# Holding GpSimd's work of a step behind the comparison of hi, and dealing the features into 20 turns over ten steps

## The chip, the cores and the metric

One core of one Trainium2 chip. The metric is the device time of one execution in microseconds (us), the median of the runs shown. The work is laid on five engines: TensorE (PE), VectorE (DVE), ScalarE (ACT), GpSimd (POOL) and SyncE (SP), the last of which here only issues DMAs.

## What is computed

Thirty-two images of 128 channels by 1024 tokens go through two layers. Cut to what matters:

```python
out = chunk_attention(q=ctx, k=ctx, v=ctx) * mask + x      # 8 heads, chunks of 64 tokens
x1 = (out - mean(out)) * rsqrt(var(out) + 1e-5)            # over the tokens
# second layer: 30 nearest neighbours of each token by ctx[:, 0:3]
idx = top_k(-squared_distance(ctx3, ctx3), 30)
rel = ctx3[idx] - ctx3                                     # 3 coordinates
rho   = sqrt(max(x*x + y*y + z*z, 1e-20))
theta = arctan2(z, sqrt(max(x*x + y*y, 1e-20)))
phi   = arctan2(y, x)
h = three small linear layers, each with batch norm over all images and a leaky relu
out = x1 + sum over neighbours of softmax(h) * x1[idx]
```

## The kernel before

The kernel has three parts. **Part 1** does the attention, the normalization, the search for the neighbours, and the angles of each neighbour ("features"). Part 2 is the three small layers, which need statistics over all images. Part 3 weights and sums the neighbours. The change is in part 1 alone.

Part 1 is a software pipeline over steps. An image has eight tiles of 128 tokens (NJ = 8), so there are S = 256 steps, and `step(s)` (L887) works on several tiles at once: the search of tile s (`distances_copy`, `eight`), the spreading of the indices of tile s-1 (`spread_indices`, with its DMAs), the comparison and gather of tile s-2 (`onehot`, `evicted`), the selection of tile s-3 (`masked`, `summed`), and the coordinates of tile s-4 (`found`, `relative`). Eleven short steps drain it. I call s modulo 8 the *phase* of a step. All of part 1 stands under `written_order`: each engine runs its instructions in the order in which the program wrote them, so a wait of one instruction holds up all that follows on its engine. Tiles come from pools with one to three buffers, and a write waits for the last reader of the buffer.

On **DVE** a step is: the maximum of the scores (L498), `eight(s, 0)`, the comparison of hi (L688), `eight(s, 1)`, a reciprocal (L510), the extras planned for s-0.5, `eight(s, 2)`, the extras planned for s, and `eight(s, 3)`. One `eight` is MAX8, FIND_INDEX8 and, but for the last, MATCH_REPLACE8 (L639 to L642) on 128x1024 float32. The comparison is one `tensor_scalar` on 128x4096 bf16, in place in the tile `hb`: the high parts of all indices of a tile against the partition's number.

On **GpSimd** a step is: `masked(s-3)` (L724, two multiplications of 128x512), `relative(s-4)` (L749, which waits for ACT's copy `got`, L742), the multiplication by the reciprocal in `normalize(s)` (L511), then the extras. `masked` needs nothing of its own step, so it starts when the extras of the step before are done.

On **ACT** a step is: eight exponentials (L502), the splitting of the indices, the copies of distances (L630), `lows` (L707, L708), copies of PSUM results, `got`, the extras of s-0.5, the copies `mk` (L714), and the extras of s.

The extras are planned by step number (L857 to L885), t0 = 8b being the first step of image b, and an x.5 means the first of the two places of a step. Among them on GpSimd: `residual` (L558, L559) in phases 5 and 1, `mask_bias` (L426) in phase 4, `norm_step` (L586 to L590) in phase 5, `split_squares` and `split_channels` (small casts and subtractions) in phase 3. On ACT: `project` (L460 and eight times L465) in phases 5 and 1, `values` (L451) and `transposed` (L609) in phase 6. On DVE: `moments1` (L565) in phases 6 and 2.

`features(b)` (L755) is a generator whose pieces, "turns", are planned one by one. Its element-wise work runs on GpSimd (on DVE for the last image), its logarithms, exponentials, sign and arctangent on ACT, and two operations with two tensor inputs (`V.scalar_tensor_tensor`, L795 and L796) and six statistics (L835, L838) on DVE. ACT loads a table wherever neighbouring instructions of its order need different ones (ACT_TABLE_LOAD). In the kernel before, 13 turns lie at t0+11.5 to t0+17.5.

Of the kernel before, what the change touches and what calls it, by code (L numbers as in the profile page):

```python
# [12 lines left out]
BF16 = mybir.dt.bfloat16  # L13
F16 = mybir.dt.float16
AF = mybir.ActivationFunctionType
ALU = mybir.AluOpType
# [7 lines left out]
TINY = 1e-20  # L24
# [31 lines left out]
def kernel(ctx: ExitStack, tc: tile.TileContext, aps: dict, out: bass.AP):  # L56
# [12 lines left out]
    nc = tc.nc  # L69
    x_d, ctx_d, mask_d = aps["x"], aps["ctx_4096"], aps["mask_Bx1x4096_ff1"]  # L70
    B, C, T = x_d.shape
# [37 lines left out]
    left = NEG  # L109
    for _ in range(3):  # L110
        m, e = math.frexp(left)
# [43 lines left out]
    least_side = column("least_side", 1e-18)  # L155
    nought_up = column("nought_up", 1e-30)
# [169 lines left out]
    with ExitStack() as part:  # L326
        p1 = part.enter_context(tc.tile_pool(name="p1", bufs=1))
        p2 = part.enter_context(tc.tile_pool(name="p2", bufs=2))
# [355 lines left out]
        def onehot(s):  # L684

            oh, lb = near[s]
            tp = per[s // NJ]["tp"]
            nc.vector.tensor_scalar(oh, oh, pcol, None, ALU.is_equal)  # L688
            pgs = []
            for r in range(2):  # L690
                pg = ps_g.tile([P, 512], F32, tag="g", name=f"ps_g_{s}_{r}")
                for i in range(3):
                    for e in range(4):
                        nc.tensor.matmul(  # L694
                            pg[e * 32 : (e + 1) * 32, :],
                            tp[:, i, :],
                            oh[:, e * 1024 + r * 512 : e * 1024 + (r + 1) * 512],
                            start=(i == 0),
                            stop=(i == 2),
                        )  # L700
                pgs.append(pg)
            near[s] = (lb, pgs)

        def lows(s):

# [13 lines left out]
        def masked(s):  # L719

            lb, mk = near[s]
            for r in range(2):
                half = mk[:, r * 4 : r * 4 + 4, :].rearrange("p k n -> p (k n)")
                nc.gpsimd.tensor_mul(half, half, lb[:, r * 512 : (r + 1) * 512])  # L724
# [30 lines left out]
        def features(b):  # L755

            rel = per[b]["rel"]
            ft = lambda tag: p1.tile([P, 2, E], F32, tag=f"f_{tag}", name=f"f_{tag}_{b}")
            half = lambda tag: p1.tile([P, E], F32, tag=f"h_{tag}", name=f"h_{tag}_{b}")

            V, G = nc.vector, nc.gpsimd if b < B - 1 else nc.vector
            sph = p2.tile([P, 3, E], F32, tag="sph", name=f"sph_{b}")
            sqr = p1.tile([P, 3, E], F32, tag="f_sqr", name=f"f_sqr_{b}")
            nc.scalar.activation(sqr, rel, AF.Square)
            ax, fy, ay = ft("ax"), ft("fy"), ft("ay")
            nc.scalar.activation(ax[:, 1, :], rel[:, 0, :], AF.Abs)
            nc.scalar.copy(fy[:, 0, :], rel[:, 2, :])
            nc.scalar.copy(fy[:, 1, :], rel[:, 1, :])
            nc.scalar.activation(ay, fy, AF.Abs)
            s2 = ft("s2")  # L770
            G.tensor_add(s2[:, 1, :], sqr[:, 0, :], sqr[:, 1, :])
            G.tensor_add(s2[:, 0, :], s2[:, 1, :], sqr[:, 2, :])
            vv, inv = ft("vv"), ft("inv")
            G.tensor_scalar(vv, s2, TINY, None, ALU.max)
            yield
            left = half("left")
            nc.scalar.activation(inv, vv, AF.Ln, scale=1024.0)
            G.tensor_scalar(left, rel[:, 0, :], 0.0, None, ALU.is_lt)
            G.tensor_scalar(s2, s2, TINY, None, ALU.is_ge)
            yield  # L780
            nc.scalar.activation(inv, inv, AF.Exp, scale=-0.5, bias=log_less)

            rr, d = ft("rr"), ft("d")
            G.tensor_mul(rr, vv, inv)
            G.tensor_mul(d, rr, rr)
            G.tensor_sub(d, vv, d)
            yield
            G.tensor_mul(d, d, inv)
            G.tensor_scalar(d, d, 0.5, None, ALU.mult)
            G.tensor_add(sph[:, 0, :], d[:, 0, :], rr[:, 0, :])  # L790

            G.tensor_add(ax[:, 0, :], d[:, 1, :], rr[:, 1, :])
            yield
            big, least, inv = ft("vv"), ft("rr"), ft("inv")
            V.scalar_tensor_tensor(big, ay, 0.0, ax, ALU.max, ALU.max)  # L795
            V.scalar_tensor_tensor(least, ay, -GONE, ax, ALU.min, ALU.min)  # L796
            nc.scalar.activation(fy, fy, AF.Sign, scale=1e20, bias=nought_up)
            nc.scalar.activation(inv, big, AF.Ln, bias=least_side)
            swap = ft("d")
            G.tensor_sub(swap, ay, ax)  # L800
            G.tensor_scalar(swap, swap, 0.0, None, ALU.is_gt)
            yield
            nc.scalar.activation(inv, inv, AF.Exp, scale=-1.0)
            t, e = ft("ay"), ft("ax")
            G.tensor_mul(t, least, inv)
            yield

            G.tensor_mul(e, t, big)
            G.tensor_sub(e, least, e)
            G.tensor_mul(e, e, inv)  # L810
            yield
            G.tensor_add(t, t, e)
            nc.scalar.activation(t, t, AF.Arctan)
            yield
            turn = ft("vv")
            G.tensor_scalar(turn, t, -2.0, PI / 2, ALU.mult, ALU.add)
            G.tensor_mul(turn, turn, swap)
            G.tensor_add(t, t, turn)
            yield
            back = half("back")  # L820
            G.tensor_scalar(back, t[:, 1, :], -2.0, PI, ALU.mult, ALU.add)
            G.tensor_mul(back, back, left)
            G.tensor_add(t[:, 1, :], t[:, 1, :], back)
            G.tensor_mul(t, t, fy)
            yield
            G.tensor_mul(sph[:, 1:3, :], t, s2)
            nc.sync.dma_start(sph_d[b].rearrange("c (p e) -> p c e", e=E), sph)
            sums = []
            for i, (u, v) in enumerate(PAIRS):
                s = p1.tile([P, E], F32, tag=f"h_s{i}", name=f"h_s{i}_{b}")  # L830
                G.tensor_add(s, sph[:, u, :], sph[:, v, :])
                sums.append(s)
            yield
            for c in range(3):
                V.bn_stats(st1[:, c, b, :], sph[:, c, :])  # L835
            yield
            for i, s in enumerate(sums):
                V.bn_stats(st1[:, 3 + i, b, :], s)  # L838

        per, proj, pairs, outs, norms, near, feats = {}, {}, {}, {}, {}, {}, {}  # L840


        extras = {}
# [1 line left out]
        def plan(step, f, *args):  # L845
            extras.setdefault(step, []).append((f, args))
# [8 lines left out]
            next(feats[b], None)  # L855

        S = B * NJ  # L857
        for b in range(B):
            t0 = b * NJ
            if b > 0:  # L860
                plan(t0 - 7, load_ctx, b)
                plan(t0 - 6, load_mask, b)
                plan(t0 + 1, load_rest, b)
                plan(t0 - 6, squares, b)
                plan(t0 - 5.5, sum_squares, b)
                plan(t0 - 5, split_squares, b)
                plan(t0 - 5, split_channels, b)
                plan(t0 - 4.5, turn_squares, b)
                plan(t0 - 4, mask_bias, b)
                plan(t0 - 3, project, b, 0)  # L870
                plan(t0 - 2, values, b)
            plan(t0 + 1, project, b, 1)
            for h in range(NH):
                done = t0 + 4 * h + 4
                plan(done, attended, b, h)
                plan(done + 1, residual, b, h)
                plan(done + 2, moments1, b, h)
            plan(t0 + 10.5, norm1, b)
            plan(t0 + 12, norm_log, b)
            plan(t0 + 12.5, norm_root, b)  # L880
            plan(t0 + 12.5, norm_step, b)
            plan(t0 + 13.5, norm4, b)
            plan(t0 + 14, transposed, b)
            for i in range(13):
                plan(t0 + 11.5 + i / 2, turn, b)  # L885

        def step(s):  # L887
            now = 0 <= s < S
            past = lambda lag: 0 <= s - lag < S
# [8 lines left out]
                spread_indices(s - 1)  # L898
            if now:
                eight(s, 0)  # L900
            if past(3):
                masked(s - 3)
            if past(1):
                turned(s - 1)
            if 0 <= s and s + 1 < S:
# [3 lines left out]
            if past(2):  # L909
                lows(s - 2)  # L910
                onehot(s - 2)
            if past(1):
                attend(s - 1)
            if past(4):
# [49 lines left out]
    with ExitStack() as part:  # L964
# [59 lines left out]
        half = NR // 2  # L1024
# [67 lines left out]
        with written_order(tc):  # L1092
# [12 lines left out]
            a2, s2 = norm(1, 1, *moments(1, 1, st2, CQ, avg_c[:, 0:CQ]), *bn2_h)  # L1105
# [28 lines left out]
    for i in range(2):  # L1134
        t = r1.tile([P, NJ, SL], F32, tag=f"pad{i}", name=f"pad{i}")
        nc.gpsimd.memset(t, 0.0)
        pads.append(t)
    for i in range(3):
        t = r1.tile([P, 4, 3, 32, NJ], BF16, tag=f"apart{i}", name=f"apart{i}")
# [114 lines left out]
    for t in range(NT):  # L1254
        b, j = t // NJ, t % NJ
# [10 lines left out]
        oh, bm = built.pop(t)  # L1266
# [58 lines left out]
```

## Time and profile before

| | us |
|---|---|
| median of 3 runs (5752.46 to 5762.36) | 5760.63 |
| the profiled execution | 5763.89 |
| its span, first to last instruction | 5762.2 |
| part 1, to the start of the last comparison of hi | 4287 |
| the drain of part 1 and the first statistics of part 2 | 58 |
| the rest of part 2, and part 3 | 1417 |
| DVE busy in part 1 | 4197 of 4287 |
| GpSimd busy in part 1 | 2331 |
| ACT busy in part 1 | 3185 |
| PE busy in part 1 | 2957 |

The profile gives the busy time of each engine, groups of equal instructions with their mean duration, and a timeline. A line of the timeline has the start in us from the span's start, the duration in us, the engine, the source line, the operation, what it writes and reads, and, in brackets, the idle time of the engine ahead of it with what ended it. The number after "x" counts instructions merged into the line. In part 1 the picture repeats image by image: from step 100 to step 108, for example, the comparisons of hi start at 1687.16, 1703.03, 1719.40, 1737.59, 1754.28, 1770.15, 1787.19, 1804.40 and 1820.28.

### The profile page before, as it was taken

The page shows a single profiled execution, that of the slowest core. Times are in us where ns is not written, and L with a number is a line of the kernel's source. Part 1 is how long each engine was busy: PE and PEld are TensorE (multiplying, and loading weights), DVE is VectorE, ACT ScalarE, POOL GpSimd, SP SyncE. Part 2 cuts the span into 40 slices and gives each one's busy share as a digit, 9 for nine tenths or more (in the row PEclk, how much of TensorE's full clock was granted, in tenths as well). Part 3 has the DMA queues.
Part 4 walks back from the last instruction along what each step waited for, and adds up shares of the span by engine and source line. Part 5 has one row for each costly group of instructions (what it writes and reads, how often), then busy time and mean ns, then how long its engine had stood idle before and what let it go on. Part 6 is the DMA issues. An engine that isn't in the chain of part 4 may idle for free. (4 is left out here: it accounts for less than half of the span.)

```text
span 5762.2 us, 126784 instructions
## 1 busy us (share of the span) xinstructions
PE 4292.3 (74%) x48908; PEld 2586.3 (45%) x48908; DVE 5289.5 (92%) x6988; ACT 4077.1 (71%) x10116; POOL 2352.9 (41%) x2725
## 2 busy tenths in 40 slices
PE   6776666776766766766776766666758679999999
PEld 3433333433333333333433334333334257777776
DVE  8999999999999999999999999999975598888876
ACT  5777777777777777777777777777764476666664
POOL 3455555555555555555555555555550000000000
PEclk8778878787878878878788878888869689999999
DMA  2222332222223322332332223323322133333332
GB/s 77 103 102 103 113 106 100 106 106 98 104 103 106 106 100 102 115 103 104 106 106 97 106 99 111 106 97 106 111 83 81 60 86 96 103 99 97 95 95 83
DMA packets 302123, 572.76 MB, mean 99 GB/s; under 512 B 139216, under 2 KB 199376, under 8 KB 268752
## 3 DMA queue, kind: packets, MB, share of 16 engines
q1 hardware_dynamic: 301520, 564.66, 29.4%
q8 instruction: 386, 6.32, 0.5%
q14 instruction: 217, 1.78, 0.1%
HBM read 439.66 MB, written 74.45 MB: 89 GB/s over the span
## 5 line engine op out<-in xcount | busy, mean ns | idle before, releaser
L639 DVE MAX8 top<-ds 128x8 f32<-128x1024 f32 x1024 | 1248.4, 1219 | 6.0 <-ACT ds L630 0.2
L640 DVE FIND_INDEX8 idx<-top,ds 128x8 uint32<-128x1024 f32 x1024 | 1248.3, 1219 | 0.0
L642 DVE MATCH_REPLACE8 ds<-top,ds 128x1024 f32<-128x1024 f32 x768 | 928.6, 1209 | 0.0
L657 PE MATMUL ps_hl<-ident,wt 128*64 128x128 f16 x256 | 74.3, 290 | 1146.0 <-ACT wt L651 1146.0
L502 ACT ACTIVATE pr<-sc,mx 128x64 f32<-128x64 f32 x2048 | 612.3, 337 | 328.7 <-DVE mx L498 323.2
L1277 PEld LDWEIGHTS <-oh 128*128 128x128 bf16 x24576 | 692.6, 96 | 334.4 <-issue 290.4
L749 POOL TENSOR_TENSOR rel<-got 128x90 f32<-128x90 f32 x256 | 99.8, 390 | 1677.5 <-ACT got L742 1600.8
L694 PE MATMUL ps_g<-hb,tp 128*32 128x512 bf16 x6144 | 649.0, 587 | 116.1 <-DVE hb L688 116.1
L1277 PE MATMUL pss<-apart,oh 128*128 128x32 bf16 x24576 | 697.2, 176 | 43.2 <-DMA apart<-bc 41.1
L724 POOL TENSOR_TENSOR mk<-mk,lb 128x512 f32<-128x512 f32 x512 | 640.6, 1271 | 3.0 <-ACT mk L714 1.0
L657 PEld LDWEIGHTS <-wt 128*64 128x64 f16 x256 | 30.8, 120 | 1338.4 <-ACT wt L651 1335.8
L1208 DVE TENSOR_TENSOR oh<-h,ihi 128x4096 bf16<-128x4096 bf16 x256 | 584.8, 2285 | 22.5 <-PE pss L1277 22.2
L731 PEld LDWEIGHTS ps_r<-sel,mk 128*128 128x128 f32 x4096 | 522.6, 207 | 181.8 <-POOL rel L749 118.3
L620 PE MATMUL pd<-cx 128*128 128x512 f32 x992 | 574.1, 663 | 0.0
L1229 PE MATMUL acc<-al,xtr 128*128 128x512 f32 x1024 | 565.7, 636 | 1.3 <-ACT al L1287 1.3
L731 PE MATMUL ps_r<-sel,mk 128*128 128x12 f32 x4096 | 546.7, 272 | 8.0 <-POOL mk L724 6.1
L502 ACT ACTIVATION_READ_ACCUMULATOR pr<-sc,mx 128x1 f32 x2048 | 471.2, 230 | 0.0
L1287 ACT COPY al<-pss 128x512 f32<-128x512 f32 x512 | 296.4, 584 | 243.7 <-PE pss L1277 240.5
L688 DVE TENSOR_SCALAR hb<-hb,pf 128x4096 bf16<-128x4096 bf16 x256 | 401.1, 1567 | 6.7 <-DMA hb<-hl 6.7
L694 PEld LDWEIGHTS <-tp 128*32 128x32 bf16 x6144 | 212.5, 130 | 432.2 <-issue 419.7
L465 ACT ACTIVATE kx<-ps_k,bkm,hmask 128x512 f32<-128x512 f32 x512 | 349.4, 788 | 11.5 <-PE ps_k L463 11.5
L1205 ACT COPY h<-hi 128x1024 bf16<-128x1024 bf16 x256 | 267.6, 1047 | 107.4 <-DVE oh L1208 105.9
(341 smaller groups left out, 8607.1 us busy)
## 6 DMA issues: line engine op xcount, KB each, us to landing
hb<-hl SPq DMA_DIRECT2D x256, 1024.0 KB
lb<-hl SPq DMA_DIRECT2D x1024, 64.0 KB
apart<-bc SPq DMA_DIRECT2D x1024, 48.0 KB
mb<-in_mask_Bx1x_ff_dram SPq DMA_DIRECT2D x32, 512.0 KB
xb<-in_x_dram SPq DMA_DIRECT2D x32, 512.0 KB
x<-xb SPq DMA_DIRECT2D x32, 512.0 KB
xt<-xt SPq DMA_DIRECT2D x32, 512.0 KB
x1r<-x SPq DMA_DIRECT2D x32, 512.0 KB
```

The source lines that it names most:

```text
L502: nc.scalar.activation(pr_t[:, i, :], sc[:, i, :], AF.Exp, bias=mx[:, i : i + 1], accum_out=sm[:, i, :],)
L620: nc.tensor.matmul(pd, cx[:, j * P : (j + 1) * P], cx[:, sl], start=True, stop=False)
L639: nc.vector.max(top[:, sl], ds)
L640: nc.vector.max_index(idx[:, sl], top[:, sl], ds)
L642: nc.vector.match_replace(ds, top[:, sl], ds, GONE)
L688: nc.vector.tensor_scalar(oh, oh, pcol, None, ALU.is_equal)
L694: nc.tensor.matmul(pg[e * 32 : (e + 1) * 32, :], tp[:, i, :], oh[:, e * 1024 + r * 512 : e * 1024 + (r + 1) * 512], start=(i == 0), stop=( ...
L724: nc.gpsimd.tensor_mul(half, half, lb[:, r * 512 : (r + 1) * 512])
L731: nc.tensor.matmul(pr.rearrange("p (e k) c -> p k e c", k=8)[:, k], mk[:, k, :], sel2, start=True, stop=True,)
L1208: nc.vector.tensor_tensor(oh.rearrange("p g a i -> p a g i"), h32.to_broadcast([P, 4, 32, 32]), ihi.to_broadcast([P, 4, 32, 32]), ALU.is_e ...
L1229: nc.tensor.matmul(acc.rearrange("p c g a -> p (c g) a"), xt[:, l, :], al[:, l], start=(l == 0), stop=(l == NJ - 1),)
L1277: nc.tensor.matmul(ps[:, k, :], oh[:, g].rearrange("p a i -> p (a i)"), bm[:, :, i, g, :], start=(i == 0), stop=(i == 2),)
```

## The change

Four edits. (1) A new `gate(s)`: GpSimd copies one element of the tile that the comparison of hi wrote into a tile of one element that nothing reads, so GpSimd's order waits there for the comparison. (2) `masked(s-3)` moves from ahead of the comparison to behind the gate. PE's, ACT's and DVE's orders are not touched by these two. (3) `features` is cut into 20 turns at other places. (4) For all images but the last, the turns are planned at t0+11, t0+11.5, ... t0+20.5; for the last, two at each place from t0+11 to t0+15.5.

I number the new turns T0 to T19. Turn i of an image falls in step t0+11 rounded up from i/2, so: phase 3 has T0 of one image and T15, T16 of the image before; phase 4 T1, T2, T17, T18; phase 5 T3, T4, T19; phase 6 T5, T6; phase 7 T7, T8; phase 0 T9, T10; phase 1 T11, T12; phase 2 T13, T14. The even turns stand in the second place of their step, the odd ones in the first.

```diff
@@ onehot @@
             nc.vector.tensor_scalar(oh, oh, pcol, None, ALU.is_equal)
+            gates[s] = oh
...
+        def gate(s):
+
+            passed = p2.tile([1, 1], BF16, tag="passed", name=f"passed_{s}")
+            nc.gpsimd.tensor_copy(passed, gates.pop(s)[0:1, 0:1])
@@ features @@
             G.tensor_add(s2[:, 0, :], s2[:, 1, :], sqr[:, 2, :])
+            yield
             vv, inv = ft("vv"), ft("inv")
             G.tensor_scalar(vv, s2, TINY, None, ALU.max)
-            yield
             left = half("left")
+            G.tensor_scalar(left, rel[:, 0, :], 0.0, None, ALU.is_lt)
+            yield
+            G.tensor_scalar(s2, s2, TINY, None, ALU.is_ge)
+            yield
             nc.scalar.activation(inv, vv, AF.Ln, scale=1024.0)
-            G.tensor_scalar(left, rel[:, 0, :], 0.0, None, ALU.is_lt)
-            G.tensor_scalar(s2, s2, TINY, None, ALU.is_ge)
             yield
             nc.scalar.activation(inv, inv, AF.Exp, scale=-0.5, bias=log_less)
 
             rr, d = ft("rr"), ft("d")
             G.tensor_mul(rr, vv, inv)
             G.tensor_mul(d, rr, rr)
+            yield
             G.tensor_sub(d, vv, d)
-            yield
             G.tensor_mul(d, d, inv)
+            yield
             G.tensor_scalar(d, d, 0.5, None, ALU.mult)
             G.tensor_add(sph[:, 0, :], d[:, 0, :], rr[:, 0, :])
 
             G.tensor_add(ax[:, 0, :], d[:, 1, :], rr[:, 1, :])
+            yield
+            nc.scalar.activation(fy, fy, AF.Sign, scale=1e20, bias=nought_up)
             yield
             big, least, inv = ft("vv"), ft("rr"), ft("inv")
             V.scalar_tensor_tensor(big, ay, 0.0, ax, ALU.max, ALU.max)
             V.scalar_tensor_tensor(least, ay, -GONE, ax, ALU.min, ALU.min)
-            nc.scalar.activation(fy, fy, AF.Sign, scale=1e20, bias=nought_up)
-            nc.scalar.activation(inv, big, AF.Ln, bias=least_side)
             swap = ft("d")
             G.tensor_sub(swap, ay, ax)
             G.tensor_scalar(swap, swap, 0.0, None, ALU.is_gt)
             yield
+            nc.scalar.activation(inv, big, AF.Ln, bias=least_side)
+            yield
             nc.scalar.activation(inv, inv, AF.Exp, scale=-1.0)
             t, e = ft("ay"), ft("ax")
             G.tensor_mul(t, least, inv)
-            yield
 
             G.tensor_mul(e, t, big)
+            yield
             G.tensor_sub(e, least, e)
             G.tensor_mul(e, e, inv)
-            yield
             G.tensor_add(t, t, e)
+            yield
+            yield
             nc.scalar.activation(t, t, AF.Arctan)
...
@@ the sums of features @@
             yield
+            yield
             for c in range(3):
                 V.bn_stats(st1[:, c, b, :], sph[:, c, :])
@@ plan @@
-            for i in range(13):
-                plan(t0 + 11.5 + i / 2, turn, b)
+
+            for i in range(TURNS):
+                plan(t0 + 11 + (i if b < B - 1 else i // 2) / 2, turn, b)
@@ step @@
                 eight(s, 0)
-            if past(3):
-                masked(s - 3)
             if past(1):
                 turned(s - 1)
...
                 lows(s - 2)
                 onehot(s - 2)
+                gate(s - 2)
+            if past(3):
+                masked(s - 3)
             if past(1):
                 attend(s - 1)
```

More of the change, by code (lines that the diff above doesn't have):

```diff
@@ L772, in features @@
             G.tensor_add(s2[:, 0, :], s2[:, 1, :], sqr[:, 2, :])
+            yield
             vv, inv = ft("vv"), ft("inv")
             G.tensor_scalar(vv, s2, TINY, None, ALU.max)
+            left = half("left")
+            G.tensor_scalar(left, rel[:, 0, :], 0.0, None, ALU.is_lt)
             yield
-            left = half("left")
+            G.tensor_scalar(s2, s2, TINY, None, ALU.is_ge)
+            yield
             nc.scalar.activation(inv, vv, AF.Ln, scale=1024.0)
-            G.tensor_scalar(left, rel[:, 0, :], 0.0, None, ALU.is_lt)
-            G.tensor_scalar(s2, s2, TINY, None, ALU.is_ge)
             yield
@@ L785, in features @@
             G.tensor_mul(d, rr, rr)
+            yield
             G.tensor_sub(d, vv, d)
+            G.tensor_mul(d, d, inv)
             yield
-            G.tensor_mul(d, d, inv)
             G.tensor_scalar(d, d, 0.5, None, ALU.mult)
@@ L805, in features @@
             G.tensor_mul(t, least, inv)
+            G.tensor_mul(e, t, big)
             yield
-            G.tensor_mul(e, t, big)
             G.tensor_sub(e, least, e)
             G.tensor_mul(e, e, inv)
+            G.tensor_add(t, t, e)
             yield
-            G.tensor_add(t, t, e)
+            yield
             nc.scalar.activation(t, t, AF.Arctan)
@@ L838, in features @@
                 V.bn_stats(st1[:, 3 + i, b, :], s)
-        per, proj, pairs, outs, norms, near, feats = {}, {}, {}, {}, {}, {}, {}
+        per, proj, pairs, outs, norms, near, feats, gates = {}, {}, {}, {}, {}, {}, {}, {}
         extras = {}
@@ L857 @@
         S = B * NJ
+        TURNS = 20
         for b in range(B):
```

## The prediction

> **What bounds the kernel now.** I read the page first: which engine is full where part 1 runs, and the group of the comparison of hi, since the gate acts on it.
>
> ```profile
> PE 4292.3 (74%) x48908; PEld 2586.3 (45%) x48908; DVE 5289.5 (92%) x6988; ACT 4077.1 (71%) x10116; POOL 2352.9 (41%) x2725
> ...
> DVE  8999999999999999999999999999975598888876
> ...
> L688 DVE TENSOR_SCALAR hb<-hb,pf 128x4096 bf16<-128x4096 bf16 x256 | 401.1, 1567 | 6.7 <-DMA hb<-hl 6.7
> ```
>
> DVE is full in the first 29 slices, and its comparison has idled only 6.7 us ahead of it, all at the drain. So DVE's order alone sets part 1's time. The chain that ended last says nothing here: it is not followed back beyond 4333 us.
>
> A mean of 1567 ns hides two kinds, so the timeline comes next: the comparisons of phases 4 to 7 of one image, and GpSimd at the slow ones.
>
> ```profile
> 1687.16 1.28 DVE L688 TENSOR_SCALAR hb<-hb,pf 128x4096 bf16<-128x4096 bf16 x1
> ...
> 1703.03 1.78 DVE L688 TENSOR_SCALAR hb<-hb,pf 128x4096 bf16<-128x4096 bf16 x1
> ...
> 1719.40 2.05 DVE L688 TENSOR_SCALAR hb<-hb,pf 128x4096 bf16<-128x4096 bf16 x1
> ...
> 1737.59 2.10 DVE L688 TENSOR_SCALAR hb<-hb,pf 128x4096 bf16<-128x4096 bf16 x1
> ```
>
> ```profile
> 1702.57 3.25 POOL L724 TENSOR_TENSOR mk<-mk,lb 128x512 f32<-128x512 f32 x2
> ...
> 1719.10 1.27 POOL L558 TENSOR_TENSOR ys<-ys,mb 128x512 f32<-128x512 f32 x1
> ...
> 1736.33 2.27 POOL L724 TENSOR_TENSOR mk<-mk,lb 128x512 f32<-128x512 f32 x2
> ```
>
> Where GpSimd is in an instruction when the comparison comes up, the comparison is longer by what is left of that instruction less 0.2 us: L558 ends at 1720.37, 0.97 after the start, and the comparison takes 2.05 for 1.28. Phases 5, 6, 7 and 1 are slow (1.78, 2.05, 2.10, 1.65), by 0.50 + 0.77 + 0.82 + 0.37 = 2.46 us an image; phases 0, 2, 3, 4 take 1.28. MAX8 and its kin keep 1219 ns throughout.
>
> **The change part by part.**
>
> *Gate, and masked behind it.* If no comparison met GpSimd, 256 x (1567 - 1278) = 74.0 us would leave DVE's order. Whether they still meet is a sum of GpSimd's step, counted from the comparison's start. The gate passes at 1.43 (1.28, and 0.15 as from the reciprocal's end at 1692.33 to L511 at 1692.48) and takes about 0.27, as norm_step's instructions do from start to start; the two multiplications of masked 2.27, to 3.97. Then relative, which waits for ACT (4.2 in phase 4), and normalize's multiplication, which waits for the reciprocal at 5.0: the extras begin at 6.3, no later than before. PE's L731 came 4.6 after the comparison's start, so masked at 3.97 costs it nothing, and its result is read a step later. Nothing else is queued behind the gate but GpSimd's own step; GpSimd issues no DMA.
>
> *The turns.* Each step's extras at their durations from start to start (1.29 for a product of 480, 0.77 of 240, 1.4 to 1.5 for a tensor_scalar). A step is 15.87; the statistics T18, T19 add 1.0 to phases 4 and 5, moments1 0.6 to phase 6.
> - Phase 3: T15 3.2, norm1 0.3, T16 3.3, T0 1.6 reach 14.6; then eleven casts and subtractions of 0.2 run to 17.6, past the comparison at 16.0. It meets one of 0.2: at most 0.05.
> - Phase 4: those leave the gate 1.5 late; T1, T2 3.6, mask_bias 3.95: 14.4 of 16.9.
> - Phase 5: T4 waits for its exponential on ACT, at 10.0 (below), then 2.4, residual 2.6: 15.0 of 16.9.
> - Phase 6: ACT is late, so relative is done at 7.5 to 8, then 1.0, T5 2.6, T6 2.8: 14.4 of 16.5.
> - Phases 7, 0, 1, 2 end by 10.5, 12.6, 12.8, 10.
>
> So every comparison is free. I keep 31 x 0.05 = 1.5 for phase 3. Between zero and the worst (phases 5 and 6 each 0.8 late) lie 0 to 50 us; the margins of 1.8 and 2.1 put it near zero.
>
> *ACT's tables.* The turns now part logarithm and exponential of one image over more places: eight loads an image for six.
>
> ```profile
> 1697.91 1.28 ACT L502 ACT_TABLE_LOAD   x1
> ...
> 1713.08 0.69 ACT L460 ACTIVATE qT<-ps_q,cols 128x512 f32<-128x512 f32 x1 [2.83 <-PE ps_q L459]
> ...
> 1719.25 0.35 ACT L502 ACTIVATE pr<-sc,mx 128x64 f32<-128x64 f32 x1
> ```
>
> ```profile
> 1715.03 0.67 DVE L498 TENSOR_REDUCE mx<-sc 128x8 f32<-128x512 f32 x1
> ```
>
> Two of them fall in phase 5, with project. Before, ACT idled 2.83 ahead of L460, and still began the exponentials of phase 6 3.55 behind their maximum (1715.70 to 1719.25). After: got ends at 4.97, norm_root 0.1, load 1.29, logarithm 0.6, mk 1.05, load 1.29, exponential 0.7: 10.0. L460 0.7 and L465 5.3 end at 16.0, the maximum at 13.2: ACT is 2.8 late. DVE would first wait at its reciprocal, if ACT were over 6.3 late. So the loads cost DVE nothing. The Trainium skill (ScalarE: Activation LUTs, "What ACT_TABLE_LOAD costs") puts a switch at 1283 ns and a drain of about 1380 more. By that, phase 5 is 2.8 longer, GpSimd's residual ends at 17.8 and the comparison of phase 6 loses 0.7 an image: 22 us more. In the trace an instruction follows 0.02 to 0.17 us after the load's end, and the load starts as the one before ends; I take 1.29.
>
> *The two operations with two inputs.* Before, L795 and L796 came in phase 6 while GpSimd waited for got: 0.61 and 0.65. In images 0 and 1 they met masked:
>
> ```profile
> 258.43 2.69 POOL L724 TENSOR_TENSOR mk<-mk,lb 128x512 f32<-128x512 f32 x2
> ...
> 258.52 1.58 DVE L795 SCALAR_TENSOR_TENSOR f_vv<-f_ay,f_ax 128x480 f32<-128x480 f32 x1
> 260.02 1.61 DVE L796 SCALAR_TENSOR_TENSOR f_rr<-f_ay,f_ax 128x480 f32<-128x480 f32 x1
> ```
>
> They alternate with it, and each loses 0.97. T8 now has them in the second place of phase 7, which DVE reaches at 8.8 (comparison 1.28, then 7.53 as in phase 6). GpSimd's own part of T8, a subtraction 1.2 and a comparison 1.4, begins behind normalize. ACT is about 1.9 late there: 2.8 from phase 5, then phase 6 takes it 15.6 (PE's ps_v holds L451), against 16.5. Relative follows 7.8 after the first exponential, which starts at 1.9 - 3.7 = -1.8: 6.0 to 6.4, normalize to 7.4, the subtraction to 8.6, the comparison of T8 8.7 to 10.1. The first operation waits for it until 9.9, about 1.05, and the second goes free. ACT 0.7 later gives 1.5, 0.7 earlier 0.6, not late at all about 0. A rule of the Trainium skill speaks for this cost and so against the change: in "SBUF — State Buffer", "Who interferes with whom", a DVE instruction with two SBUF inputs contends with a GpSimd instruction that reads SBUF. The rows show it for products; that it holds for T8's tensor_scalar as well rests on the rule, and by the rows alone the cost is 0. I take 1.0 x 31 = 31 us, less 4 x 0.97 = 3.9 that images 0 and 1 paid before: +27. Bounds: -4 (none) and +55 (1.9 an image).
>
> *SP and the drain.* The write of sph is now issued in phase 3, where T16's product ends near 11; the next in SP's queue, the index write, comes at about 13. Hidden, with 2 us of cover; beyond it the read of hb landed 5.8 us or more before its comparison. In the drain, image 30's turns on GpSimd (T10 to T16) precede the last relative, but the last residual and products did so before; ACT waits for T16 ahead of the absolute value, some 1 us. I take 0, between -3 and +3.
>
> **Sum.** -74.0 + 1.5 + 27 + 0 = -45.5 on the profiled 5763.9 gives 5718; that run stands 3.3 over the median, so 5715.
>
> **Rivals.**
> - *The two operations go free* (ACT less late in phase 7, or a tensor_scalar does not hold DVE): -74 + 1.5 - 4 = -76, 5685 to 5690. For it: a shift of 1.4 us in ACT is enough. Against: ACT's lag of 3.5 in that phase before.
> - *More collisions, still faster*: both operations wait (1.5 to 1.9), or phase 6 loses 0.5: 5731 to 5750.
> - *Slower*: GpSimd's steps in phases 4, 5 and 6 outlast the next comparison, each losing what is left of one instruction, 0.8 on average. It decides once GpSimd is 2.5 us later than summed. With the two operations at 1.0, 3.4 an image stands against 2.46: 31 x 0.94 - 4 = +25, 5786. For it: GpSimd must now do in 14.4 us what had the whole step. Against: it has idle time behind the gate until 5.0 in any case.
> - *It does nothing*: losses equal the gain, 2.4 an image; 5755 to 5765.
>
> **How the numbers follow.** Chances: forecast 0.50, free 0.25, more collisions 0.11, nothing 0.05, slower 0.09. The range, 5686 to 5748, takes in the free case and most of the collisions. Faster by over 0.2% (11.5 us, about what a measurement of this kernel tells from no change) 0.86, within it 0.05, slower 0.09.
>
> **What would show it.** L688 near 1285 ns in the mean; L795 and L796 together near 2.25 for 1.26, in phase 7, with L801's successor beside them; eight loads of 1283 an image, and no DVE idle time ahead of the reciprocal; an image's eight comparisons 131.7 us apart for 133.1. Wrong would be: comparisons of phases 5 or 6 still over 1.5, or waits of DVE for ACT.

## The result, and the profile after

The changed kernel takes 5701.65 us (median of 4 runs, 5698.45 to 5710.01), beside 5761.49 for the kernel before, which now has four runs as well: a ratio of 0.9897, 95% interval 0.9875 to 0.9918. The profiled execution took 5698.45, that is 65.4 less than the profiled one of before. The forecast was 5715, with 5718 for the profiled one; its rival "the two operations go free" was 5685 to 5690. The time lies between the two.

| stage, us | before | after | difference |
|---|---|---|---|
| 1st comparison of hi to the 255th | 4216.4 | 4147.2 | -69.3 |
| last comparison of hi to the first batch-norm statistics of part 2 (drain) | 46.8 | 50.8 | +4.0 |
| from there to the end (parts 2 and 3) | 1428.6 | 1428.5 | -0.1 |

The first row is the steady part of part 1, and the following is judged by it. The page shows the same occupation of DVE as before, and 256 more instructions on GpSimd (POOL), which are the gates:

```profile
PE 4295.8 (75%) x48908; PEld 2597.9 (46%) x48908; DVE 5220.7 (92%) x6988; ACT 4169.0 (73%) x10178; POOL 2349.4 (41%) x2981
...
DVE  8999999999999999999999999999975598888876
...
L708 POOL COPY passed<-hb 1x1 bf16<-1x1 bf16 x256 | 45.8, 179 | 1098.1 <-DVE hb L688 1098.1
```

GpSimd spends 1098.1 us, 4.3 a step, standing at the gate. DVE's busy time fell by 68.8 us. Why it fell is in the row of the comparison, shown here by its line, before and after (minimum, median and maximum of the duration in ns; "x128" at the end counts only the sample whose shape was read):

```profile
L688 DVE TENSOR_SCALAR hb<-hb,pf x256: 1275/1279/2159, 61.6 to 4286.8; 128x4096 bf16<-128x4096 bf16 x128
...
L688 DVE TENSOR_SCALAR hb<-hb,pf x256: 1267/1278/1286, 60.9 to 4217.4; 128x4096 bf16<-128x4096 bf16 x128
```

After the change the longest of 256 takes 1286 ns. Before, 123 of them were slow, and their sum was 401.1; now it is 327.1.

The timeline of phases 4 to 7 answers to the four comparisons shown of before; GpSimd's gate stands behind each. In all the timelines below, rows of other instructions that lie between those shown are left out.

```profile
1660.05 1.28 DVE L688 TENSOR_SCALAR hb<-hb,pf 128x4096 bf16<-128x4096 bf16 x1
...
1676.72 1.28 DVE L688 TENSOR_SCALAR hb<-hb,pf 128x4096 bf16<-128x4096 bf16 x1
1678.06 0.18 POOL L708 COPY passed<-hb 1x1 bf16<-1x1 bf16 x1 [2.49 <-DVE hb L688]
1678.33 2.27 POOL L730 TENSOR_TENSOR mk<-mk,lb 128x512 f32<-128x512 f32 x2
...
1693.46 1.28 DVE L688 TENSOR_SCALAR hb<-hb,pf 128x4096 bf16<-128x4096 bf16 x1
1694.81 0.18 POOL L708 COPY passed<-hb 1x1 bf16<-1x1 bf16 x1 [3.09 <-DVE hb L688]
...
1709.80 1.28 DVE L688 TENSOR_SCALAR hb<-hb,pf 128x4096 bf16<-128x4096 bf16 x1
1711.14 0.18 POOL L708 COPY passed<-hb 1x1 bf16<-1x1 bf16 x1 [3.81 <-DVE hb L688]
```

In the brackets is what GpSimd had left when its step was done: 2.49, 3.09 and 3.81 us up to the start of the gate, which follows the comparison's end by 0.06. So it stopped 1.15, 1.75 and 2.47 us before the comparison's start.

The two operations with two inputs are the cost that was forecast. Three images in a row, at the second place of phase 7, give three different answers. Image 11:

```profile
1716.62 1.20 POOL L809 TENSOR_TENSOR f_d<-f_ay,f_ax 128x480 f32<-128x480 f32 x1
...
1717.91 1.41 POOL L810 TENSOR_SCALAR f_d<-f_d 128x480 f32<-128x480 f32 x1
1718.70 0.65 DVE L806 SCALAR_TENSOR_TENSOR f_vv<-f_ay,f_ax 128x480 f32<-128x480 f32 x1
1719.26 0.65 DVE L807 SCALAR_TENSOR_TENSOR f_rr<-f_ay,f_ax 128x480 f32<-128x480 f32 x1
```

Image 12:

```profile
1848.43 1.20 POOL L809 TENSOR_TENSOR f_d<-f_ay,f_ax 128x480 f32<-128x480 f32 x1
1849.29 0.86 DVE L806 SCALAR_TENSOR_TENSOR f_vv<-f_ay,f_ax 128x480 f32<-128x480 f32 x1
1849.72 1.69 POOL L810 TENSOR_SCALAR f_d<-f_d 128x480 f32<-128x480 f32 x1
1850.07 1.03 DVE L807 SCALAR_TENSOR_TENSOR f_rr<-f_ay,f_ax 128x480 f32<-128x480 f32 x1
```

Image 13:

```profile
1980.20 1.41 POOL L810 TENSOR_SCALAR f_d<-f_d 128x480 f32<-128x480 f32 x1
1980.47 0.83 DVE L806 SCALAR_TENSOR_TENSOR f_vv<-f_ay,f_ax 128x480 f32<-128x480 f32 x1
1981.22 0.65 DVE L807 SCALAR_TENSOR_TENSOR f_rr<-f_ay,f_ax 128x480 f32<-128x480 f32 x1
```

In image 11 L806 begins while L810, a tensor_scalar, has still 0.62 us to run, and takes 0.65 all the same. In image 13 it begins 0.27 behind L810's start and takes 0.83; with 0.65 of work it was held until 1980.65, which is 0.45 behind L810's start. In image 12 it meets the subtraction and is held 0.21. L810 in turn begins while L806 runs and takes 1.69 for 1.41, so it is held itself, by 0.28; and L807 meets the first part of this L810 and is held to 0.73 behind its start, which is 0.45 and the 0.28. So this tensor_scalar holds a DVE operation with two inputs, but for its first 0.45 us of 1.41 only. Other images give 0.44 where the operation begins 0.10, 0.11 and 0.23 behind L810 (0.99, 0.98, 0.86 us), and 0.45 where it begins 0.42 behind (0.68). Over 32 images L806 and L807 take 51.1 us, L795 and L796 took 44.4 before: +6.7, where +27 was forecast.

### The profile page after: what moved, and what is told of

The parts are those of the page before. It is cut to its first block, busy times and chain, and to the rows that moved or that the text cites. A ratio compares the mean times of both kernels' runs of the same rounds, so it can differ in the third digit from the quotient of the medians.

```text
span 5696.7 us, 127167 instructions
## 1 busy us (share of the span) xinstructions
PE 4295.8 (75%) x48908; PEld 2597.9 (46%) x48908; DVE 5220.7 (92%) x6988; ACT 4169.0 (73%) x10178; POOL 2349.4 (41%) x2981
## 5 line engine op out<-in xcount | busy, mean ns | idle before, releaser
L695 PE MATMUL ps_g<-hb,tp 128*32 128x512 bf16 x6144 | 625.2, 569 | 79.6 <-DVE hb L688 79.6
L730 POOL TENSOR_TENSOR mk<-mk,lb 128x512 f32<-128x512 f32 x512 | 582.4, 1158 | 17.4 <-ACT pts L522 1.1
L708 POOL COPY passed<-hb 1x1 bf16<-1x1 bf16 x256 | 45.8, 179 | 1098.1 <-DVE hb L688 1098.1
L480 PE MATMUL sc<-kx,qT 128*64 128x512 f32 x1024 | 330.1, 727 | 8.6 <-ACT kx L465 5.6
```

The costliest lines, as they stand in the source:

```text
L695: nc.tensor.matmul(pg[e * 32 : (e + 1) * 32, :], tp[:, i, :], oh[:, e * 1024 + r * 512 : e * 1024 + (r + 1) * 512], start=(i == 0), stop=( ...
```

## The experiments

The following table is from two chips, each kernel beside runs of the kernel before on its own chip: the first four beside a median of 5769.3, the last four beside 5770.7. "Steady" is the span from the first comparison to the 255th, against 4216.4 before and 4147.2 after; "two inputs" is the sum of the two operations, "comparisons" the sum of L688 (us, one profiled execution each).

| kernel | median | ratio, 95% interval | steady | comparisons | two inputs | drain |
|---|---|---|---|---|---|---|
| gate alone | 5726.3 | 0.9923 [0.9906, 0.9939] | 4165.6 | 351.5 | 42.2 | 45.6 |
| turns alone | 5728.1 | 0.9918 [0.9901, 0.9934] | 4164.3 | 344.2 | 51.4 | 50.8 |
| two inputs early | 5703.5 | 0.9879 [0.9862, 0.9895] | 4140.6 | 326.8 | 42.0 | 50.6 |
| product for tensor_scalar | 5727.4 | 0.9920 [0.9904, 0.9937] | 4163.1 | 327.1 | 67.3 | 50.3 |
| tensor_scalar for subtraction | 5704.8 | 0.9886 [0.9872, 0.9900] | 4145.7 | 327.1 | 50.1 | 50.3 |
| two more loads | 5777.3 | 1.0015 [1.0006, 1.0024] | 4211.3 | 359.3 | 83.5 | 53.3 |
| two inputs early, drain dealt | 5702.5 | 0.9888 [0.9873, 0.9902] | 4146.1 | 327.4 | 42.8 | 40.2 |
| the change again | 5716.4 | 0.9911 [0.9894, 0.9929] | 4146.2 | 326.8 | 50.8 | 50.5 |

The last row is the same code as the changed kernel. Its steady part is within 1 us of the first profile's; its median stands 14.8 higher, its six executions range from 5702.90 to 5730.82, and of its profiled execution parts 2 and 3 take 10 us more (1438.7 for 1428.5), though nothing there differs. That remainder lies between 1428.5 and 1447.9 us among these ten profiles. So a difference of under 20 us between two of these medians says little, and what a cause of a few us does is read from the steady part. The 1 us between the two profiles of the change is all that is known of that part's own scatter.

**Gate alone.** The kernel before with edits (1) and (2), and the 13 old turns at their old places.

```diff
-            if past(3):
-                masked(s - 3)
...
+                gate(s - 2)
+            if past(3):
+                masked(s - 3)
```

> The kernel before with the gate, and masked behind it; the 13 turns stay as they were. Theory A (a comparison loses what is left of the GpSimd instruction that runs when it comes up, and nothing else): the slow comparisons of phases 5, 7 and 1 met masked, which is now behind the gate, so they fall to 1.28; in phase 6 residual still stands in the way and it keeps 2.05. Saved 2.46 - 0.77 = 1.69 us an image, 51 us in all: about 5713 in the profile. Theory B (with the old turns the gate pushes GpSimd's step past the next comparison in phases 5 to 7 as well): three slow phases remain, under 20 us saved, 5745 or more.

The steady part is 50.8 below the kernel before, where theory A had 51. Phases 5, 7 and 1 are free, and phase 6 alone is left, at a mean of 2.04. The timeline of one phase 6, GpSimd's `residual` and the comparison:

```profile
1698.42 1.26 POOL L558 TENSOR_TENSOR ys<-ys,mb 128x512 f32<-128x512 f32 x1
1698.53 2.24 DVE L688 TENSOR_SCALAR hb<-hb,pf 128x4096 bf16<-128x4096 bf16 x1
```

GpSimd is in `residual` of phase 5 when the next comparison comes; the comparison takes 2.24, which is 1.28 and the 1.15 that L558 still ran, less 0.2. The gate orders a step behind the comparison, but a step that is too long for its slot runs into the next one. That is what the new turns take away.

**Turns alone.** The changed kernel without the gate (`masked` stays behind the comparison in the program, where nothing holds it).

```diff
-                gate(s - 2)
```

> The changed kernel without the gate's copy; GpSimd's written order is otherwise that of the changed kernel, and masked again starts as soon as the extras of the step before are done. Theory A: masked takes 2.27 us, and in the changed kernel the extras end 0.4 to 2.6 us ahead of the comparison in phase 5, 1.75 in phase 6, 2.3 in phase 7 and over 2.6 elsewhere; so phases 5 and 6 are slow in part, by about 0.5 and 0.3, phases 7 and 1 at most a little: 20 to 25 us over the changed kernel, 5715 to 5728. Theory B (the gate is what does it, the turns are worth nothing by themselves): 5750 or more.

The steady part is 52.2 below before and 17.1 above the change: phase 5 is at 1.56 in the mean, phase 6 at 1.49, and elsewhere two single comparisons are slow (2.01 and 2.12). That is theory A, a little under its 20 to 25. The gate brings 50.8, the turns 52.2, both together 69.3. They are no two sums to be added: both take the collisions of the same phases away.

**Two inputs early.** The two operations in T7, the first place of phase 7, behind T7's Sign on ACT and ahead of T8's subtraction and comparison on GpSimd.

```diff
             nc.scalar.activation(fy, fy, AF.Sign, scale=1e20, bias=nought_up)
-            yield
-            big, least, inv = ft("vv"), ft("rr"), ft("inv")
+            big, least = ft("vv"), ft("rr")
             V.scalar_tensor_tensor(big, ay, 0.0, ax, ALU.max, ALU.max)
             V.scalar_tensor_tensor(least, ay, -GONE, ax, ALU.min, ALU.min)
+            yield
+            inv = ft("inv")
             swap = ft("d")
```

> The changed kernel with the two operations of two inputs moved from T8 to T7, the first place of phase 7, where GpSimd waits for got. Theory A (their extra 10.7 us in all is time lost to GpSimd's subtraction and comparison of T8): they sum to 40 to 44 us instead of 51.1, and the kernel is 7 to 11 us faster than the changed one: 5688 to 5692. Theory B (they are slower for another reason): their sum stays near 51 and the time at 5698.

The sum of the two falls to 42.0, near the price of 64 free ones, and the steady part by 6.5 against the change's first profile (5.6 against its second). That is most of what the collision costs in the changed kernel: the early place is not wholly free, since in nine images the second operation takes 0.84 beside the subtraction of `relative`. The whole time cannot tell it: this ratio's interval overlaps the change's own of either chip.

**Product for tensor_scalar.** The same change with GpSimd's second operation of T8 made a product. It leaves out the flag that says whether y and x are swapped.

```diff
-            G.tensor_scalar(swap, swap, 0.0, None, ALU.is_gt)
+            G.tensor_mul(swap, swap, ax)
```

> The changed kernel with the tensor_scalar of T8 on GpSimd replaced by a product of two tensors of the same size, so that the swap flag of the angles is left out and the output is not the reference's. Theory A (GpSimd instructions with two tensor inputs hold a two-input operation of DVE to their end, tensor_scalar hardly does): the two operations sum to 60 to 75 us instead of 51.1 and the time rises by 10 to 20 us: 5708 to 5720. Theory B (tensor_scalar holds it just as long, and they meet less than I worked out): no change, 5698, or a little less since a product is 0.2 us shorter.

The two operations take 67.3 and the steady part is 15.9 longer than the change's. An image of the kind in which both meet GpSimd:

```profile
1985.91 1.19 POOL L809 TENSOR_TENSOR f_d<-f_ay,f_ax 128x480 f32<-128x480 f32 x1
1986.47 1.15 DVE L806 SCALAR_TENSOR_TENSOR f_vv<-f_ay,f_ax 128x480 f32<-128x480 f32 x1
1987.18 1.50 POOL L810 TENSOR_TENSOR f_d<-f_d,f_ax 128x480 f32<-128x480 f32 x1
1987.54 1.65 DVE L807 SCALAR_TENSOR_TENSOR f_rr<-f_ay,f_ax 128x480 f32<-128x480 f32 x1
```

L807 begins 0.36 behind the product's start and is held to 1988.54, 0.14 before the product's end. In the changed kernel the same meeting cost L807 0.38 (1.03, image 12). So the kind of operation on GpSimd decides: a product holds DVE nearly to its end, this tensor_scalar does not. That the product reads `ax`, as the two operations do, is not the reason: `masked` shares no tile with them and held them in images 0 and 1 of the kernel before, and in the next run a tensor_scalar that reads `ay` with them does not hold them to its end.

**tensor_scalar for subtraction.** T8's first operation becomes a tensor_scalar too, and the second is again the comparison with 0. It leaves out the difference of y and x.

```diff
-            G.tensor_sub(swap, ay, ax)
+            G.tensor_scalar(swap, ay, 0.5, None, ALU.mult)
```

> The changed kernel with GpSimd's subtraction of T8 replaced by a tensor_scalar of the same size, so that both its instructions there are tensor_scalars of 1.4 us; the difference behind the swap flag is left out, and the output is not the reference's. Theory A (a tensor_scalar of GpSimd does not hold a two-input operation of DVE once it runs): the two operations sum to 40 to 44 us instead of 51.1, and from the first comparison of hi to the 255th it takes 4137 to 4142 us instead of 4147. Theory B (it holds it as a product does): they run to 10.3 us behind the comparison, so the two operations meet them in every image and sum to 60 or more, and that stretch takes 4156 or more.

Neither: 50.1 for the two operations, and a steady part only 1.5 below the change's. The timeline of one image:

```profile
1846.89 1.41 POOL L809 TENSOR_SCALAR f_d<-f_ay 128x480 f32<-128x480 f32 x1
...
1848.38 1.41 POOL L810 TENSOR_SCALAR f_d<-f_d 128x480 f32<-128x480 f32 x1
1848.53 0.94 DVE L806 SCALAR_TENSOR_TENSOR f_vv<-f_ay,f_ax 128x480 f32<-128x480 f32 x1
1849.40 0.64 DVE L807 SCALAR_TENSOR_TENSOR f_rr<-f_ay,f_ax 128x480 f32<-128x480 f32 x1
```

L806 begins 0.15 behind L810 and is held 0.29: again to 0.44 behind its start. L807, 1.02 behind it, goes free though L810 has 0.39 to run. Over all images of this run the operation is free where it begins 0.5 or more behind a tensor_scalar that started undisturbed, and is held to 0.44 or 0.45 behind it where it begins earlier. (All of those held met L810, the comparison with 0. An undisturbed L809, the product with 0.5, was met only from 0.50 on.) So both theories failed, each in one half of the instruction: held in the first 0.45, not held after. With two tensor_scalars there are two such windows to run into, which is why the sum did not fall.

**Two more loads.** Two activations of one column each, ahead of T4's exponential in phase 5, so that ACT loads its tables twice more an image. Nothing reads what they write.

```diff
+            nc.scalar.activation(spare, spare_in, AF.Exp)
+            nc.scalar.activation(spare, spare_in, AF.Ln)
             nc.scalar.activation(inv, inv, AF.Exp, scale=-0.5, bias=log_less)
...
```

> The changed kernel with two more table loads an image on ACT in phase 5, ahead of T4's exponential (a logarithm and an exponential of one column that nothing reads): 2.8 us more on ACT an image. Theory A (my sums): ACT is 5.5 late at the start of phase 6, short of the 6.3 at which DVE would wait at its reciprocal; residual ends 0.9 to 1.0 behind the start of the comparison of phase 6, which rises to about 2.0; and in phase 7 the two operations meet products instead of the tensor_scalar, 0.3 to 0.9 more. In all 0.8 to 1.4 us an image: 25 to 45 us over the changed kernel from the first comparison to the 255th (4172 to 4192). Theory B (a load costs 2.66 us): DVE waits at the reciprocal of phase 6, 4240 or more. Theory C (ACT is hidden, loads are free): 4147 to 4152.

The way it goes was expected, its size was not: +64 in the steady part. T4 waits 3 us longer, and GpSimd's `residual` comes into the comparison of phase 6:

```profile
1712.46 1.27 POOL L558 TENSOR_TENSOR ys<-ys,mb 128x512 f32<-128x512 f32 x1
...
1713.80 1.27 POOL L559 TENSOR_TENSOR xb<-xb,ys 128x512 f32<-128x512 f32 x1
1713.81 2.34 DVE L688 TENSOR_SCALAR hb<-hb,pf 128x4096 bf16<-128x4096 bf16 x1
```

That gives 32.2 (359.3 for 327.1). The other half, 32.4, is in the two operations of T8: with ACT 4.05 late in phase 7, where 1.9 was summed, `normalize`'s multiplication and the subtraction of T8 run beside them, and from image 2 to image 29 they take 1.08 to 1.16 and 1.65. Both sums together are the 64 that the steady part lost. DVE still waits for no reciprocal, though ACT's lag in phase 6 has risen from 2.8 to 5.8, so theory B (the load with the drain that the prediction named) did not come. The profit of the change hangs on less than 3 us of ACT: with two loads more the kernel is no faster than before.

**Two inputs early, drain dealt.** The early place, and the last image but one dealt two turns a place like the last, so that its turns don't lie on GpSimd in the drain.

```diff
-                plan(t0 + 11 + (i if b < B - 1 else i // 2) / 2, turn, b)
+                plan(t0 + 11 + (i if b < B - 2 else i // 2) / 2, turn, b)
```

> The changed kernel with the two operations of two inputs in T7, and the last image but one dealt two turns a place as the last is. Theory A: from the first comparison to the 255th 4140 to 4145 us (that image meets two or three comparisons again), and the drain from the last comparison to the first statistic of part 2 falls from 50.8 to 45 to 48 us, because the last image's absolute value no longer waits for T16 of the image before: 8 to 12 us faster than the changed kernel beside it. Theory B (the drain is longer for another reason): it stays near 50.8.

The drain falls by 10.4 against the early place alone, to 40.2, below the kernel before; but the steady part's end gives 5.5 back. There, in image 30, DVE waits 4.47 for a turn of GpSimd, and the second operation then takes 1.65 for 0.65:

```profile
4166.05 0.66 DVE L805 SCALAR_TENSOR_TENSOR f_vv<-f_ay,f_ax 128x480 f32<-128x480 f32 x1 [4.47 <-POOL f_ax L801]
4166.63 1.65 DVE L806 SCALAR_TENSOR_TENSOR f_rr<-f_ay,f_ax 128x480 f32<-128x480 f32 x1
```

From the 255th comparison to the last it takes 3.4 longer besides. The end of the drain comes 1.4 earlier than with the early place alone, at 4259.9 for 4261.3 us, and 8 earlier than in the changed kernel (4268.2). The ratio of 0.9888 is not told apart from the change's 0.9911 on the same chip: their intervals overlap.

**The change again.**

> The changed kernel once more, beside the others on one chip: ratio to the kernel before 0.988 to 0.992; from the first comparison to the 255th within 1 us of 4147.2; parts 2 and 3 may differ by up to 20 us, as they did among the runs so far, for a reason that is not in part 1.

It shows which part of a difference between chips is the kernel's: none of the 10 us in parts 2 and 3.

## Why the prediction was right, and where it was not

The time lies in the range, and the gain and its main cost are those that were forecast. But the sum was 19.9 short (-45.5 for -65.4), and more than all of that is one term, the two operations. The range took in the rival in which they go free, so that the time lies in it says little for this term. A part was luck: without the 4.0 of the drain, which was not foreseen, the miss would have been near 24.

*The comparisons.* Forecast -74.0, measured -74.0. The sums of GpSimd's steps held where they were tightest: its step of phase 5 ends 1.75 to 1.9 ahead of the next comparison (1.8 forecast), that of phase 6 2.23 to 2.47 (2.1). The step of phase 4 has less room than the 2.5 that its 14.4 of 16.9 gave: from 0.39 to 2.66, as it falls; it was nearest to a collision and had none. That of phase 2 ends at 11.8 to 13.7 for a forecast 10, which costs nothing. Gate alone confirms the cause from the other side: with the old turns the collision stays in just the phase whose step is too long.

*Phase 3 meets the small casts: +1.5.* Measured 0. They are still running when the comparison comes, but it is GpSimd that waits:

```profile
1660.05 1.28 DVE L688 TENSOR_SCALAR hb<-hb,pf 128x4096 bf16<-128x4096 bf16 x1
1660.28 1.12 POOL L417 CAST tp<-tf 128x24 bf16<-128x24 f32 x1
1661.47 0.23 POOL L419 TENSOR_TENSOR tf<-tf,tp 128x24 f32<-128x24 f32 x1
1661.77 0.20 POOL L417 CAST tp<-tf 128x24 bf16<-128x24 f32 x1
```

The cast issued 0.23 behind the comparison's start takes 1.12 for 0.20. The gate passes late by as much as the casts take (phase 4), which costs nothing.

*ACT's tables: 0.* Right. Eight loads of 1283 ns an image, no wait of DVE ahead of the reciprocal in the steady part, ACT 2.65 to 2.81 late at the start of phase 6 where 2.8 was forecast, and 1.34 to 2.49 in phase 7 for 1.9. The Trainium skill's drain of about 1380 ns beside each load ("ScalarE: Activation LUTs", "What ACT_TABLE_LOAD costs") would have made phase 5 some 2.8 longer. It did not appear here, nor in the run with two more loads, where ACT became 3.0 later for 2.57 of loads and two small activations.

*The two operations with two inputs: +27.* Here lies the error; the place and the mechanism were right, the size was not. The step that failed is "the first operation waits for it until 9.9, about 1.05": it took from the rule of the Trainium skill ("SBUF — State Buffer", "Who interferes with whom"), by which such a DVE instruction contends with a GpSimd instruction that reads SBUF, that this tensor_scalar holds DVE too, and from the products of before for how long, to its end less 0.2. That it contends is so; the runs show it for 0.45 us from its start. The operations come, as forecast, while GpSimd is in its part of T8; they lose 0 in one kind of image, 0.18 in another, and 0.59 in the third, where L806 meets the subtraction and L807 meets L810's first part: 0.26 an image, and 0.31 with the less regular first images, for 1.0. By the rows alone the prediction said 0 (the rival, 0.25), by the rule 1.05; the truth was neither. Over 31 images their durations make it 9.5 us, and the early place gave 6.5 back, against the 31 of the prediction. With these for 31 and 0 for the casts the sum is -74.0 + 9.5 - 3.9 = -68.4 or -74.0 + 6.5 - 3.9 = -71.4, beside the measured -69.3.

*The drain: 0, between -3 and +3.* Measured +4.0. Image 30's last turns on GpSimd hold the last image's first ones more than the second that was taken for them. The timeline at the end of part 1:

```profile
4238.46 1.20 POOL L836 TENSOR_TENSOR f_ay<-f_ay,f_fy 128x480 f32<-128x480 f32 x1
4239.69 0.39 ACT L773 COPY f_fy<-rel 128x240 f32<-128x240 f32 x1 [2.07 <-POOL f_ay L836]
...
4239.92 1.20 POOL L838 TENSOR_TENSOR sph<-f_ay,f_s 128x480 f32<-128x480 f32 x1
4241.15 0.60 ACT L775 ACTIVATE f_ay<-f_fy 128x480 f32<-128x480 f32 x1 [0.78 <-POOL sph L838]
4241.15 0.41 DVE L777 TENSOR_TENSOR f_s<-f_sqr 128x240 f32<-128x240 f32 x1 [9.71 <-POOL sph L838]
```

ACT stands 2.07 for L836 and 0.78 for L838, which free the buffers of fy and ay: the prediction named "some 1 us" of it. Dealing that image's turns closer took the drain down by 10.4, which shows that it is their place that lengthens it.

*The rivals.* "The two operations go free" (5685 to 5690) came true for 1 image of 3. "Slower" was given a threshold of 2.5 us of GpSimd; two more loads, which bring T4 3 us later, cross it and cost 64, or 2.1 an image beyond the change, where that rival had 2.4. But of its three phases only one collided, at 1.04; the other half came by the two operations. "More collisions" and "it does nothing" didn't come.

## What to carry to other kernels

A wait on one element of another engine's result is a cheap way (0.18 us an instruction, and here nothing on the path) to order two engines that disturb each other, but it does not help where a step is too long for its slot and runs into the next one: sum each step to its end. Where DVE is full, price a collision by the kind of instruction on both sides and by what is running when the DVE instruction comes, since here a product and a tensor_scalar held it for different lengths, and where DVE's instruction began first it was GpSimd that waited (a cast took 1.12 for 0.20). Judge a change of a few us by the stage that it touches, where the whole time wanders by more.

## What the runs showed that was not expected

- GpSimd's tensor_scalar on 128x480 float32 holds a two-input DVE operation for its first 0.45 us of 1.41, for the comparison with 0, in the changed kernel and in the run with two tensor_scalars alike; the product with 0.5 let it go from 0.50 on. What it does in those 0.45 us no row shows. A product or a subtraction of the same size takes 1.20 and holds for about 1.05 of it.
- The image's time is not the same from image to image: 130.59, 131.18 and 130.77 us, over and over. The differences are what the two operations lose, 0, 0.59 and 0.18. The granted TensorE clock repeats with them. Phase 6 of images 11 to 15, in one view of the changed kernel (us, then busy time of PE, PEld, DVE, ACT, POOL with counts, then the granted clock, DMA share and GB/s):

```profile
1693.46:1709.80 16.34, 12.37 (x146) 7.83 (x146) 16.10 (x23) 14.32 (x49) 8.97 (x10) 0.84 0.41 148
1824.05:1840.38 16.33, 13.65 (x146) 8.28 (x146) 16.09 (x23) 13.14 (x39) 8.99 (x10) 0.76 0.41 148
1955.24:1971.57 16.33, 12.89 (x146) 8.01 (x146) 16.09 (x23) 13.90 (x45) 8.98 (x10) 0.81 0.42 148
2085.99:2102.34 16.35, 12.37 (x146) 7.84 (x146) 16.11 (x24) 14.33 (x49) 8.98 (x10) 0.84 0.43 148
2216.59:2232.92 16.33, 13.64 (x146) 8.29 (x146) 16.09 (x23) 13.15 (x39) 8.98 (x10) 0.76 0.42 148
```

The clock is 0.84, 0.76, 0.81 and again 0.84, 0.76. In the image with 0.76 PE is 1.28 us longer busy, ACT is 2.45 late in phase 7 for 1.34, and the two operations meet the subtraction. The clock's climb does not come from the collisions: with the two operations early, two or three images in a row take the same 130.62 us, and one in every three or four 130.81; and through such a row the clock of the same stretch still rises (images 12 to 15):

```profile
1819.99:1836.32 16.33, 13.69 (x145) 8.29 (x146) 16.09 (x24) 13.03 (x38) 8.99 (x10) 0.75 0.43 148
1950.60:1966.94 16.34, 13.45 (x145) 8.21 (x146) 16.10 (x24) 13.28 (x41) 8.98 (x10) 0.78 0.40 148
2081.22:2097.55 16.33, 12.82 (x145) 7.98 (x146) 16.09 (x23) 13.89 (x45) 8.97 (x10) 0.81 0.44 149
2211.83:2228.16 16.33, 12.37 (x145) 7.83 (x146) 16.09 (x23) 14.23 (x49) 8.97 (x10) 0.84 0.40 148
```

ACT's lag in phase 7 goes with the clock there too, 2.64 at 0.75 and 1.34 to 1.37 at 0.84. So these rows speak for this order: the clock comes first, ACT's lag goes with it, and the lag decides which collision an image has. In the kernel before and with two more loads, where an image takes 133.1 us, the clock of that stretch stays the same from image to image (0.81 and 0.71 to 0.72, from the third on). No run sets the clock by itself, and why it climbs at 130.6 us an image and stands still at 133.1 stays open.
- Parts 2 and 3, untouched in all of these kernels, took 1428.5 to 1447.9 us. These runs don't show why.
